# A MoE layer on one core: first rows of expert 2 moved ahead, and down products of row block pairs by seven products

## The chip, the core and the metric

One core of a Trainium2 chip. The time is the device time in microseconds of one execution. The engines named below are TensorE (PE; its weight loads are shown as PEld), VectorE (DVE), ScalarE (ACT), GpSimd (POOL) and SyncE (SP), which here only issues transfers.

## The reference

Input x is 8 sequences of 512 tokens with 256 numbers each, in f32. Two residual layers follow, and all weights are f32.

```python
# layer 1: attention, a convolution over the sequence, and attention again with the result as query
x = x + attn(layernorm(x))
# layer 2, on z = layernorm(x), returned as a whole and added to x:
h = z + attention(rmsnorm(z))          # 16 heads, rotary positions, causal
y = h + moe(rmsnorm(h))
def moe(x):                            # 8 experts, 2 per token, hidden width 704
    probs = softmax(x @ w_router)
    topw, topi = top_k(probs, 2); topw = topw / sum(topw)
    combine = sum(one_hot(topi) * topw)
    g = silu(einsum('td,xdh->txh', x, wg)); u = einsum('td,xdh->txh', x, wu)
    eo = einsum('txh,xhd->txd', g * u, wd)
    return einsum('txd,tx->td', eo, combine)
```

The change touches only the MoE. The kernel computes for each expert only the tokens that chose it.

## The kernel before

**Stages.** Up to about 865 us the kernel works through the attention layers of the eight batches. As a batch is routed, its rows are scattered by POOL (indirect DMAs, L1877) into a table `xtab` in DRAM, which has 1152 places (CAP) for each expert. Then, for each expert, rows are loaded from the table, multiplied, and added into the output by indirect DMAs from POOL (`send`, L985 to L1006). A row holds 256 numbers, its token number and its shares.

**Half experts.** An expert's rows are worked in two halves: (e, 0) has 512 rows, four row blocks of 128; (e, 1) has 608 rows, four blocks and one of 96. `places` (L2201) is the order of the halves: (0,0), then (1,0), (1,1), (2,0), (2,1) and so on to (7,1), and (0,1) last. Expert 0's first half and most of (1,0) are interleaved with the last two batches. `load_rows` (L796) is given to SP one place ahead; the rows of (1,1) can be read only when all scatters have landed. The first halves of experts 0 and 1 are read earlier, and the kernel counts with `early` and `needed` (L1134, L1858 to L1861, L1025) that enough rows of them were there; otherwise another, general path is taken at the end.

**A half.** `make(n)` transposes the rows on TensorE (L859, L866), and ScalarE brings them out of PSUM (L862, L872). `mixed_rows` adds them up in four combinations on VectorE. Then five groups k = 0..4 of 128 hidden columns, and a tail of 64. A group (L908 to L946) computes gate and up together, a 2x2 block product, by seven products instead of eight, named p1, p6, p5, p7, p1, p5, p7 in their order; each of p1, p5, p7 is read by VectorE or ScalarE between its first and its second product, which adds into the same PSUM bank. VectorE makes u, v, v and then c12, u; ScalarE makes the silu; POOL multiplies into `hT` (L943, L944). A group is cut in two by `yield`, so that other work can stand in the middle. The weights' combinations come from `mixed_weights` (eight VectorE operations per expert).

**Down products.** In the loop over n (L2246), group k of half n has in its middle `down(k)` of half n-1 (L969): one row block, six matmuls 128x256 over the hidden dimension into a PSUM bank ("bank": two of "mm", two of "av", in turn). ScalarE multiplies by the row's share (L983). The tail of half n comes after group 4. `spare` puts a few of the waiting VectorE operations after each part. POOL sends two row blocks at k = 1, one each at k = 2 and 3, and the fifth at the end. The last send of a half waits until the others have landed, and the next half's first waits for that one (`unordered`, L729).

**What sets the order.** PE, ACT, DVE and POOL run in the order in which the program lists their work (a manual schedule, L2046); SP's transfers are placed by the planner. The tiles are few: four PSUM banks "g0" to "g3" for groups and tail in turn, two buffers of p, three of u, two of v, two sets of weights (experts of even and odd number), three of rows.

Of the kernel before, what the change touches and what calls it, by code (L numbers as in the profile page):

```python
# [11 lines left out]
F32 = mybir.dt.float32  # L12
I32 = mybir.dt.int32
AF = mybir.ActivationFunctionType
ALU = mybir.AluOpType
# [679 lines left out]
def fast_path(  # L695
# [118 lines left out]
    def mixed_weights(gu, mixed):  # L814
# [13 lines left out]
            ]  # L828
        return ops

    class Half:


# [135 lines left out]
        def down(self, s):  # L969
# [12 lines left out]
            to = self.shares[s] = self.share[:m, s % 2, :]  # L982
            nc.scalar.mul(to, po, self.share_of(s)[:m])  # L983

        def send(self, n=1):  # L985

            for _ in range(n):
                s = len(self.sent)
                m = self.rows[s][1]
                self.sent.append(  # L990
                    nc.gpsimd.indirect_dma_start(  # L991
                        out=out,
                        out_offset=bass.IndirectOffsetOnAxis(
                            ap=self.rows[s][0][:m, D : D + 1].bitcast(I32), axis=0
                        ),
                        in_=self.shares[s][:m],
                        in_offset=None,
                        bounds_check=B * S - 1,
                        oob_is_err=False,
                        compute_op=ALU.add,  # L1000
                    ).ins
                )
# [40 lines left out]
    with ExitStack() as att:  # L1043
# [86 lines left out]
        for e in range(NE):  # L1130
            nc.gpsimd.memset(order[:, e : e + 1], float(NE - e))
            nc.gpsimd.memset(run[:, e : e + 1], float(e * CAP))
            nc.gpsimd.memset(limit[:, e : e + 1], float((e + 1) * CAP))
        for i, n in enumerate((FIRST, FIRST, CAP + FIRST)):  # L1134
            nc.gpsimd.memset(needed[:, i : i + 1], float(n))
        token = wp.tile([P, NT], I32, tag="token", name="token")
        nc.gpsimd.iota(token, pattern=[[P, NT]], base=0, channel_multiplier=1)
# [321 lines left out]
        class Batch:  # L1459
# [383 lines left out]
            def slots(self):  # L1843

                b = self.b
                at = small.tile(full, F32, tag="at", name="at", bufs=2)
                slot = small.tile([P, NC, 2], I32, tag="slot", name="slot", bufs=3)
                rest, red, rows = self.rest, self.red, self.rows

                ps = mm_tile()  # L1850
                n = NC * NE
                flat = self.both.rearrange("p c e -> p (c e)")
                nc.tensor.matmul(ps[:, :n], before, flat, start=True, stop=True)
                nc.tensor.matmul(ps[:, n : 2 * n], every, flat, start=True, stop=True)
                for c in range(NC):
                    nc.vector.tensor_tensor(at[:, c, :], run, ps[:, c * NE : (c + 1) * NE], ALU.add)
                    nc.vector.tensor_tensor(run, run, ps[:, n + c * NE : n + (c + 1) * NE], ALU.add)
                if b == B - 3:  # L1858
                    nc.vector.tensor_copy(early[:, 0:1], run[:, 0:1])
                if b == B - 2:  # L1860
                    nc.vector.tensor_copy(early[:, 1:3], run[:, 0:2])  # L1861

                nc.vector.tensor_tensor(rest, at, limit.unsqueeze(1).to_broadcast(full), ALU.is_ge)
                nc.vector.scalar_tensor_tensor(at, rest, float(2 * NE * CAP), at, ALU.mult, ALU.add)
                for k, pick in enumerate(self.pick):
                    nc.vector.tensor_mul(pick, pick, at)  # L1866
# [179 lines left out]
        with tc.manual_schedule(  # L2046
# [26 lines left out]
            def room(what):  # L2073
                i = next(turns_of[what])
                if what[:7] == "weights":
                    if what not in rooms:
                        first = what == "weights0"
                        gu = [
                            pool.tile([P, 2 * HID], F32, tag=tag, name="gu", bufs=1)
                            for pool, tag in (  # L2080
                                ((wp, "conv"), (wp, "wqkv_sb"))
                                if first
                                else ((big, "kT1"), (wp, "va1"))
                            )
                        ]
# [4 lines left out]
                        mixed_dn = None  # L2090
                        rooms[what] = gu, mixed, dn, mixed_dn
                    return rooms[what]
                if what == "rows":
# [19 lines left out]
                    return small.tile([P, S], F32, tag="t0", name="u", bufs=3)  # L2113
                if what == "v":
                    return wp.tile([P, S], F32, tag=("cosT", "sinT")[i % 2], name="v")
                if what == "share":
                    return big.tile([P, 2, D], F32, tag=f"cs{i % 2}", name="share")
                if what == "pgu":
# [79 lines left out]
            load_up(1, weights[1][0])  # L2198
            load_down(1, weights[1][2])
            t.rms()  # L2200
            places = [(0, 0)] + [(e, i) for e in range(1, NE) for i in range(2)] + [(0, 1)]  # L2201
            rows = {1: load_rows(room, *places[1])}
            half.tail()
            while any(due.values()):
                for where in due:
                    follow_up(where)
# [37 lines left out]
            spare(of_rows, 4)  # L2244
            halves[1].tail()
            for n in range(2, len(places) + 1):  # L2246
# [2 lines left out]
                if n + 1 < len(places):  # L2249
                    rows[n + 1] = load_rows(room, *places[n + 1])  # L2250
                if n == 2:
                    to_mix += mixed_weights(*weights[2][:2])
                if now and n > 2 and i == 0:
                    more = (e + 1) % NE
                    load_up(more, weights[more][0])
                    next_mix = mixed_weights(*weights[more][:2])
                if now and n > 2 and i == 1:
                    to_mix, next_mix = next_mix, []
                for k in range(NK - 1):
                    if now:  # L2260
                        group = now.group(k)
                        next(group)
                        spare(to_mix, 2)
                    if k == 2 and n + 1 < len(places):
                        of_rows = make(n + 1)
                    if k < len(done.rows):
                        done.down(k)
                    if k in (1, 2, 3):
                        done.send(2 if k == 1 else 1)
                    if now:  # L2270
                        next(group)
                        spare(to_mix, 1)
                    if k == 2:
                        to_mix += of_rows if n + 1 < len(places) else []
# [4 lines left out]
                if now and n > 2 and i == 0:  # L2279
# [54 lines left out]
```

## Time and profile before

| | us |
|---|---|
| median of three runs (1397.76 to 1402.78) | 1398.43 |
| the profiled execution | 1395.17 |
| its span, first to last instruction | 1393.4 |

The mean granted TensorE clock of this execution is 0.991 of full speed. The slices of the page for the other engines, 40 of 34.8 us each:

```profile
PEld 5566555666555566556565564558777878778775
DVE  5754896875896765886665865335645454544541
ACT  4677777777777776786776785323233333333331
POOL 3344334556334556333555334324444454544444
PEclk9999999999999999999999999989999999999998
```

Each digit is the busy share in tenths; PEclk is the granted clock. The MoE alone begins near slice 25. A group of instructions in the views below is given with its line, engine, operation, tiles (out<-in), shape and count. Durations of matmuls overlap[...]; the distance between starts is what one costs. A matmul in f32 has two records in the trace.

### The profile page before, as it was taken

The page shows a single profiled execution, that of the slowest core. Times are in us where ns is not written, and L with a number is a line of the kernel's source. Part 1 is how long each engine was busy: PE and PEld are TensorE (multiplying, and loading weights), DVE is VectorE, ACT ScalarE, POOL GpSimd, SP SyncE. Part 2 cuts the span into 40 slices and gives each one's busy share as a digit, 9 for nine tenths or more (in the row PEclk, how much of TensorE's full clock was granted, in tenths as well). Part 3 has the DMA queues.
Part 4 walks back from the last instruction along what each step waited for, and adds up shares of the span by engine and source line. Part 5 has one row for each costly group of instructions (what it writes and reads, how often), then busy time and mean ns, then how long its engine had stood idle before and what let it go on. Part 6 is the DMA issues. An engine that isn't in the chain of part 4 may idle for free. (4 is left out here: it accounts for less than half of the span.)

```text
span 1393.4 us, 33183 instructions
## 1 busy us (share of the span) xinstructions
PE 1338.5 (96%) x13564; PEld 908.6 (65%) x13564; DVE 856.9 (61%) x1760; ACT 789.4 (57%) x1346; POOL 628.2 (45%) x637
## 2 busy tenths in 40 slices
PE   8999999999999999999999999879999999999997
PEld 5566555666555566556565564558777878778775
DVE  5754896875896765886665865335645454544541
ACT  4677777777777776786776785323233333333331
POOL 3344334556334556333555334324444454544444
PEclk9999999999999999999999999989999999999998
DMA  5222122211001211001212023423232333333211
GB/s 143 70 83 87 67 79 82 74 40 60 17 25 55 75 43 59 13 25 39 84 50 86 13 88 93 127 53 74 57 73 55 89 85 70 73 59 79 56 17 21
DMA packets 65281, 88.50 MB, mean 64 GB/s; under 512 B 12640, under 2 KB 46624, under 8 KB 65120
## 3 DMA queue, kind: packets, MB, share of 16 engines
q1 hardware_dynamic: 51840, 68.94, 14.9%
q0 software_dynamic: 13280, 17.35, 7.4%
q8 instruction: 108, 1.77, 0.6%
q14 instruction: 53, 0.43, 0.1%
HBM read 36.35 MB, written 31.82 MB: 49 GB/s over the span
## 5 line engine op out<-in xcount | busy, mean ns | idle before, releaser
L1423 ACT ACTIVATE pr<-sc 128x1024 f32<-128x1024 f32 x432 | 418.8, 1024 | 136.9 <-PE sc L1416 131.7
L1431 POOL TENSOR_TENSOR pr<-pr,seen 128x512 f32<-128x512 f32 (+1 forms) x216 | 257.5, 1192 | 390.2 <-ACT pr L1423 380.8
L1346 PE MATMUL av<-pr,va 64*32 64x512 f32 (+7 forms) x6144 | 216.3, 407 | 0.0
L1416 PE MATMUL sc<-qT,kT 32*128 32x320 f32 (+7 forms) x2048 | 192.5, 434 | 6.4 <-ACT pr L1423 6.3
L1346 PEld LDWEIGHTS av<-pr,va 64*32 64x32 f32 x6144 | 112.1, 106 | 101.5 <-issue 78.2
L1376 DVE RECIPROCAL r<-r 128x256 f32<-128x256 f32 x96 | 167.4, 1744 | 9.8 <-DMA r<-cs 9.8
L923 PE MATMUL pgu<-xgT,gu 128*128 128x304 f32 (+1 forms) x560 | 170.7, 403 | 0.0
L1416 PEld LDWEIGHTS sc<-qT,kT 32*128 32x128 f32 x2048 | 116.2, 184 | 80.9 <-ACT pr L1423 34.5
L812 DVE TENSOR_TENSOR u<-u,pgu 128x304 f32<-128x304 f32 (+1 forms) x140 | 62.9, 449 | 167.9 <-PE pgu L923 160.7
L991 POOL DMA_INDIRECT out_dram<-share,xg x64 | 102.7, 1605 | 138.0 <-ACT share L983 129.9
L812 POOL TENSOR_TENSOR hT<-p,u 128x304 f32<-128x304 f32 (+1 forms) x70 | 80.0, 1142 | 129.7 <-DVE u L812 129.7
L923 PE MATMUL pgu<-xgT,mixed 128*128 128x304 f32 (+1 forms) x420 | 135.6, 404 | 0.4 <-DVE v L812 0.4
L923 PEld LDWEIGHTS pgu<-xgT,gu 128*128 128x128 f32 x560 | 105.6, 190 | 31.4 <-issue 3.3
L973 PE MATMUL po<-dn,hT 128*128 128x256 f32 (+1 forms) x444 | 102.1, 380 | 0.0
L973 PE MATMUL mm<-dn,hT 128*128 128x256 f32 (+1 forms) x420 | 97.0, 380 | 1.6 <-ACT xgT L862 1.6
L1416 PE MATMUL sc<-q2T,kT 32*128 32x512 f32 (+7 forms) x1024 | 93.0, 434 | 0.7 <-ACT pr L1423 0.5
L923 PEld LDWEIGHTS pgu<-xgT,mixed 128*128 128x128 f32 x420 | 78.4, 190 | 21.5 <-DVE hT L812 3.5
L973 PEld LDWEIGHTS po<-dn,hT 128*128 128x128 f32 (+1 forms) x444 | 82.0, 186 | 13.9 <-issue 0.2
L936 ACT ACTIVATE p<-pgu 128x304 f32<-128x304 f32 (+1 forms) x70 | 28.5, 407 | 108.1 <-PE pgu L923 104.0
L973 PEld LDWEIGHTS mm<-dn,hT 128*128 128x128 f32 (+1 forms) x420 | 78.3, 188 | 15.3 <-ACT xgT L862 2.9
L1877 POOL DMA_INDIRECT xtab<-rows,slot x64 | 64.9, 1014 | 35.5 <-DVE pick L1866 18.9
L1416 PEld LDWEIGHTS sc<-q2T,kT 32*128 32x128 f32 x1024 | 58.3, 184 | 32.6 <-issue 14.4
(210 smaller groups left out, 1967.7 us busy)
## 6 DMA issues: line engine op xcount, KB each, us to landing
r<-cs SPq DMA_DIRECT2D x96, 128.0 KB, 2.0
xtab<-pad SPq DMA_DIRECT2D x24, 397.5 KB, 3.5
xg<-xtab SPq DMA_DIRECT2D x16, 530.0 KB, 3.7
gu<-in_wg_dram SPq DMA_DIRECT2D x18, 352.0 KB, 4.5
cs<-cs SPq DMA_DIRECT2D x48, 128.0 KB, 1.9
gu<-in_wu_dram SPq DMA_DIRECT2D x18, 320.0 KB, 3.9
dn<-in_wd_dram SPq DMA_DIRECT2D x9, 640.0 KB, 5.1
out_dram<-x SPq DMA_DIRECT2D x8, 512.0 KB, 3.0
```

The costliest lines, as they stand in the source:

```text
L812: engine.tensor_tensor(out, a, b, op)
L923: nc.tensor.matmul(ps, lhsT, rhs, start=start, stop=True, skip_group_check=not start)
L936: nc.scalar.activation(p, p1, AF.Silu)
L973: nc.tensor.matmul(po, self.hidden(k)[:, s * P : s * P + m], self.dn[:, k, :], start=(k == 0), stop=(k == NK - 1),)
L991: nc.gpsimd.indirect_dma_start(out=out, out_offset=bass.IndirectOffsetOnAxis(ap=self.rows[s][0][:m, D : D + 1].bitcast(I32), axis=0), in_= ...
L1346: nc.tensor.matmul(av[i][g * HP : (g + 1) * HP, j * KB :], v[rows, j, ch * G + g, :], pr[rows, g, at : at + n], start=(j == 0), stop=(j == ...
L1376: nc.vector.reciprocal(r[:, half], r[:, half])
L1416: nc.tensor.matmul(sc[:, g - g0, at : at + S - j * KB], kT[r0 : r0 + HP, ch, j], qT[r0 : r0 + HP, ch, j * KB : S], start=True, stop=True,)
L1423: nc.scalar.activation(pr[:, g0 : g0 + 2], sc, AF.Exp, scale=SCALE)
L1431: nc.gpsimd.tensor_tensor(diag, diag, seen.unsqueeze(1).unsqueeze(1).to_broadcast([P, G, len(parts), KB]), ALU.mult,).ins
L1877: nc.gpsimd.indirect_dma_start(out=xtab, out_offset=bass.IndirectOffsetOnAxis(ap=slot[:, c, k : k + 1], axis=0), in_=rows[:, c, :], in_off ...
```

## The change

The order of places becomes (0,0), (1,0), (2,0), (1,1), (2,1), (3,0) and on as before. The rows of (1,0) and (2,0) are loaded together, before the last batch is routed; the counts that are asked of early rows become those of experts 0, 1 and 2. Expert 2's weights are loaded and mixed earlier, expert 1's weights are mixed one half later, and expert 3's are loaded at turn 4.

From turn 3 to turn 15 the row blocks 0 to 3 of the half before are taken in pairs. Two row blocks by the two halves of the hidden dimension (3 x 128 each) are multiplied with `wd`'s four quarters by seven products of 3 matmuls 128x128x128. Four sums of the hidden values per pair (`mixed_hidden`) and four of `wd` per expert (`mixed_down`) are made first. The pairs stand in groups 1 and 3, a fifth row block in group 4; row blocks are sent one each at k = 1 to 4. The tail moves from behind group 4 to behind group 0.

```diff
+    def mixed_down(dn, mixed):
+        t1, t2, t3, t4 = (mixed[:, n] for n in range(4))
+        b11, b12 = dn[:, :3, :P], dn[:, :3, P:]
+        b21, b22 = dn[:, 3:, :P], dn[:, 3:, P:]
+        return [
+            lambda: tt(nc.gpsimd, t1, b12, b11, ALU.subtract),
+            lambda: tt(nc.gpsimd, t2, b22, t1, ALU.subtract),
+            lambda: tt(nc.gpsimd, t3, b22, b12, ALU.subtract),
+            lambda: tt(nc.gpsimd, t4, b21, t2, ALU.subtract),
+        ]
...
+        def mixed_hidden(self, pair):
+            engine = (nc.vector, nc.gpsimd)[pair]
+            two_each = [self.room("hs") for _ in range(2)]
+            s = self.hs[pair] = [t[:, n] for t in two_each for n in range(2)]
...
+            a11, a21, a12, a22 = h1[:, :, one], h1[:, :, two], h2[:, :, one], h2[:, :, two]
+            return [
+                lambda: tt(engine, s[0], a21, a22, ALU.add),
+                lambda: tt(engine, s[1], s[0], a11, ALU.subtract),
+                lambda: tt(engine, s[2], a11, a21, ALU.subtract),
+                lambda: tt(engine, s[3], a12, s[1], ALU.subtract),
+            ]
+        def down_pair(self, pair):
...
+            p1, p6, p5, p7 = (self.room("bank")[:, :P] for _ in range(4))
...
+            def product(ps, lhsT, rhs, start=True):
+                for k in range(3):
+                    nc.tensor.matmul(ps, lhsT[:, k], rhs[:, k], start=(start and k == 0), stop=(k == 2), ...)
+            product(p1, side(h1, one), b11)
+            nc.scalar.copy(p, p1)
+            product(p6, s2, t2)
+            tt(nc.vector, u, p, p6, ALU.add)
+            product(p5, s1, t1)
+            tt(nc.vector, v, u, p5, ALU.add)
+            product(p7, s3, t3)
+            tt(nc.vector, share[:, 1, P:], v, p7, ALU.add)
+            product(p1, side(h2, one), b21, False)
+            nc.scalar.mul(share[:, 0, :P], p1, w1)
+            product(p5, s4, b22, False)
+            tt(nc.vector, share[:, 0, P:], u, p5, ALU.add)
+            nc.scalar.mul(share[:, 0, P:], share[:, 0, P:], w1)
+            product(p7, side(h2, two), t4, False)
+            tt(nc.vector, share[:, 1, :P], u, p7, ALU.add)
+            nc.scalar.mul(share[:, 1, :], share[:, 1, :], w2)
...
-        for i, n in enumerate((FIRST, FIRST, CAP + FIRST)):
+        for i, n in enumerate((FIRST, CAP + FIRST, 2 * CAP + FIRST)):
...
-                    nc.vector.tensor_copy(early[:, 1:3], run[:, 0:2])
+                    nc.vector.tensor_copy(early[:, 1:3], run[:, 1:3])
...
-            places = [(0, 0)] + [(e, i) for e in range(1, NE) for i in range(2)] + [(0, 1)]
-            rows = {1: load_rows(room, *places[1])}
+            places = [(0, 0), (1, 0), (2, 0), (1, 1), (2, 1)]
+            places += [(e, i) for e in range(3, NE) for i in range(2)] + [(0, 1)]
+            rows = {n: load_rows(room, *places[n]) for n in (1, 2)}
             half.tail()
+            load_up(2, weights[2][0])
...
-            load_up(2, weights[2][0])
             load_down(2, weights[2][2])
-            rows[2] = load_rows(room, *places[2])
-            to_mix = mixed_weights(*weights[1][:2])
+            to_mix = mixed_weights(*weights[2][:2])
             halves[1].plain_group(2)
+            spare(to_mix, 4)
+            of_rows = make(2)
             halves[1].plain_group(3)
             spare(to_mix, 4)
-            of_rows = make(2)
...
+                more = 3 if n == 4 else (e + 1) % NE
+                fresh = now and (n == 4 or n > 4 and i == 0)
+                if fresh:
                     load_up(more, weights[more][0])
                     next_mix = mixed_weights(*weights[more][:2])
...
+                pairs = now and n > 2
...
+                mix_down = {2: 2, 3: 1, 5: 3}.get(n, more if now and n > 5 and i == 1 else None)
...
                 for k in range(NK - 1):
                     if now:
                         group = now.group(k)
                         next(group)
-                        spare(to_mix, 2)
+                        spare(to_mix, 1)
                     if k == 2 and n + 1 < len(places):
                         of_rows = make(n + 1)
-                    if k < len(done.rows):
-                        done.down(k)
-                    if k in (1, 2, 3):
+                    if not pairs:
+                        if k < len(done.rows):
+                            done.down(k)
+                    elif k in (1, 3):
+                        done.down_pair(k // 2)
+                    elif k == 4 and len(done.rows) > 4:
+                        done.down(4)
+                    if not pairs and k in (1, 2, 3):
                         done.send(2 if k == 1 else 1)
                     if now:
                         next(group)
-                        spare(to_mix, 1)
...
+                        if k == 0:
+                            now.tail()
+                        if pairs and k == 0:
+                            spare(done.mixed_hidden(0), 4)
+                            spare(done.mixed_hidden(1), 4)
+                        else:
+                            spare(to_mix, 2)
+                    if pairs and k in (1, 3):
+                        done.send(1)
+                    if pairs and k in (2, 4):
+                        done.send(1)
+                    if k > 1:
+                        spare(downs, 2)
+                    to_mix += of_rows
...
                 spare(to_mix, len(to_mix))
-                if now:
-                    now.tail()
                 done.send(len(done.rows) - 4)
```

`hs` has four buffers of two sums each, `sums` two buffers of three 128x128 tiles; `mixed_dn` is one tile for each of the two weight sets.

More of the change, by code (lines that the diff above doesn't have):

```diff
@@ L983, in down @@
             nc.scalar.mul(to, po, self.share_of(s)[:m])
+        def mixed_hidden(self, pair):
+            engine = (nc.vector, nc.gpsimd)[pair]
+            two_each = [self.room("hs") for _ in range(2)]
+            s = self.hs[pair] = [t[:, n] for t in two_each for n in range(2)]
+            one = slice(2 * pair * P, (2 * pair + 1) * P)
+            two = slice((2 * pair + 1) * P, (2 * pair + 2) * P)
+            h1, h2 = self.hT[0], self.hT[1]
+            a11, a21, a12, a22 = h1[:, :, one], h1[:, :, two], h2[:, :, one], h2[:, :, two]
[5 more added lines that the diff above has]
+            ]
@@ new lines, in down_pair, with side @@
+        def down_pair(self, pair):
+            one, two = 2 * pair, 2 * pair + 1
+            h1, h2 = self.hT[0], self.hT[1]
+            def side(h, s):
+                return h[:, :, s * P : (s + 1) * P]
+            s1, s2, s3, s4 = self.hs[pair]
+            t1, t2, t3, t4 = (self.mixed_dn[:, n] for n in range(4))
+            b11, b21, b22 = self.dn[:, :3, :P], self.dn[:, 3:, :P], self.dn[:, 3:, P:]
+            p1, p6, p5, p7 = (self.room("bank")[:, :P] for _ in range(4))
+            sums = self.room("sums")
+            p, u, v = (sums[:, n, :] for n in range(3))
+            share = self.room("share")
+            w1, w2 = self.share_of(one), self.share_of(two)
+            def product(ps, lhsT, rhs, start=True):
+                for k in range(3):
+                    nc.tensor.matmul(
+                        ps,
+                        lhsT[:, k],
+                        rhs[:, k],
+                        start=(start and k == 0),
+                        stop=(k == 2),
+                        skip_group_check=not start,
+                    )
+            product(p1, side(h1, one), b11)
[14 more added lines that the diff above has]
+            nc.scalar.mul(share[:, 1, :], share[:, 1, :], w2)
+            self.shares[one], self.shares[two] = share[:, 0, :], share[:, 1, :]
@@ L2089, in room @@
                         nc.gpsimd.memset(dn[:TAIL, HT, :], 0.0)
-                        mixed_dn = None
+                        pool, tag, bufs = (wp, "va0", 1) if first else (big, "pr", 5)
+                        mixed_dn = pool.tile([P, 4, 3, P], F32, tag=tag, name="mixed_dn", bufs=bufs)
                         rooms[what] = gu, mixed, dn, mixed_dn
@@ L2115, in room @@
                     return wp.tile([P, S], F32, tag=("cosT", "sinT")[i % 2], name="v")
+                if what == "sums":
+                    return big.tile([P, 3, P], F32, tag="r", name="sums")
+                if what == "hs":
+                    return keep.tile([P, 2, 3, P], F32, tag="x", name="hs", bufs=4)
                 if what == "share":
@@ L2251, in fast_path @@
                 if n == 2:
-                    to_mix += mixed_weights(*weights[2][:2])
-                if now and n > 2 and i == 0:
-                    more = (e + 1) % NE
+                    to_mix = mixed_weights(*weights[1][:2])
+                more = 3 if n == 4 else (e + 1) % NE
+                fresh = now and (n == 4 or n > 4 and i == 0)
+                if fresh:
                     load_up(more, weights[more][0])
                     next_mix = mixed_weights(*weights[more][:2])
-                if now and n > 2 and i == 1:
+                if now and n > 4 and i == 1:
                     to_mix, next_mix = next_mix, []
+                pairs = now and n > 2
+                of_rows = []
+                mix_down = {2: 2, 3: 1, 5: 3}.get(n, more if now and n > 5 and i == 1 else None)
+                if mix_down is None:
+                    downs = []
+                else:
+                    downs = mixed_down(*weights[mix_down][2:])
                 for k in range(NK - 1):
@@ L2271, in fast_path @@
                         next(group)
-                        spare(to_mix, 1)
-                    if k == 2:
-                        to_mix += of_rows if n + 1 < len(places) else []
+                        if k == 0:
[3 more added lines that the diff above has]
+                            spare(done.mixed_hidden(1), 4)
+                        else:
+                            spare(to_mix, 2)
[6 more added lines that the diff above has]
+                    to_mix += of_rows
+                    of_rows = []
+                    if k == 1 and n == 4:
+                        to_mix, next_mix = next_mix, []
                 spare(to_mix, len(to_mix))
-                if now:
-                    now.tail()
                 done.send(len(done.rows) - 4)
-                if now and n > 2 and i == 0:
+                if fresh:
                     load_down(more, weights[more][2])
```

## The prediction

> **What bounds the kernel now.** I read the shares and slices of the page first, then the MoE stretch by stage, then TensorE in order of time, then groups by shape.
>
> ```profile
> PE 1338.5 (96%) x13564; PEld 908.6 (65%) x13564; DVE 856.9 (61%) x1760; ACT 789.4 (57%) x1346; POOL 628.2 (45%) x637
> ...
> PE   8999999999999999999999999879999999999997
> ```
>
> TensorE is the bound everywhere but in two dents, one at its end and one in slices 26 to 28. The windows (us of PE, PEld, DVE, ACT, POOL, then granted clock, DMA share, GB/s) of the second dent, and of one later half expert, show why:
>
> ```profile
> 900.90:914.00 13.10, 0.04 (x1) 0.00 (x0) 2.87 (x5) 0.00 (x0) 5.37 (x6) 0.63 0.40 110
> 914.00:917.50 3.50, 3.47 (x12) 2.63 (x13) 0.00 (x0) 1.84 (x4) 0.00 (x0) 0.50 0.39 149
> ...
> 1149.00:1180.00 31.00, 30.66 (x142) 25.33 (x141) 13.12 (x29) 10.27 (x25) 14.60 (x15) 1.00 0.34 81
> ```
>
> In a half expert TensorE has no free time and every other engine has half of it. So what TensorE saves there is won, and what makes it wait there is lost. TensorE in order of time (start, us until the last one ends, count, and the idle time before it):
>
> ```profile
> 886.74 0.39 PE L1854 MATMUL mm<-both,every 128*128 128x32 f32 x2
> 886.96 13.98 PE L897 MATMUL pgu<-xgT,gu 128*128 128x512 f32 x32
> 914.03 1.97 PE L859 MATMUL mm<-ident,xg 128*128 128x128 f32 x8 [13.09 <-DMA xg<-xtab]
> ...
> 937.45 1.04 PE L859 MATMUL mm<-ident,xg 128*128 128x128 f32 x8
> 938.32 2.75 PE L973 MATMUL po<-dn,hT 128*128 128x256 f32 x12
> 940.91 0.68 PE L923 MATMUL pgu<-xgT,mixed 128*128 128x304 f32 x2
> ```
>
> [...]A down product's row block is 12 records in 2.59 us, 0.216 each (six matmuls in f32, two records each). A 304-wide product is two in 0.51.
>
> **Part A: first rows of expert 2 before the rest of expert 1.** Before, the rows of (1,1) are loaded only when the last batch's scatters have landed: POOL issues the last at 907.9, SP issues the row load at 910.4, TensorE gets it at 914.0. It waits 13.09 us, and then runs 3.5 us at a granted clock of 0.50 and 3.5 at 0.94: 3.5 x 0.50 + 3.5 x 0.06 = 1.96 us more. The rows of (2,0) are loaded with those of (1,0) at about 869, behind scatters that are already out, so (2,0) takes the idle place; (1,1) is asked for three group turns later, near 922, and its rows land near 914 as before. What the step moves with it: six weight loads of expert 2 (SP shows them already at 870 to 873), eight mixing operations, which go to a VectorE that was busy 2.87 of those 13.1 us, and expert 3's loads, which now have one half expert (30 us) before use where others have two; six loads of some 4 us each, side by side, are covered by that; uncovered they would cost up to 8. A VectorE burst of three left-over mixing operations at the end of (2,1) may cost 1 us or so. **A gives 15.0 us.** That it only moves the wait is a rival below.
>
> **Part B, gain on TensorE.** Thirteen half experts (the turns 3 to 15) compute two pairs each by products: 7 x 3 matmuls 128 wide, 42 records, in place of 2 x 12 of 256. No row has a 128-wide f32 product with full weights. From below: the transposes at 937.45 are 128 wide, each with its own weights, 0.87/8 = 0.109 apart. From above: the 32-wide pair at 886.74, whose stream is short, so that only the weight load can pace it, is 0.11 apart. I take 0.1105: 42 x 0.1105 = 4.64 against 24 x 0.216 = 5.18. Saved 0.54 a pair, 26 pairs: **14.1 us** (12.5 to 15.6). Here a rule speaks against the change: the Trainium skill, "TensorE: Matmul & The Clock Gate", Part 3, "The mechanism", says a weight load overlaps running matmuls only where its row group differs. Load (by its "LDWEIGHTS", 128/1.2 = 107 ns) and stream would then add up to 0.216 for each 128-wide record, an estimate: 42 x 0.216 = 9.07, a loss of 3.9 a pair, 101 us in all. The transposes at 0.109, full rows, contradict it; I follow the row.
>
> **Part B, what it adds elsewhere.** Per pair: five VectorE operations on PSUM 128 wide, near 0.29 us by the slope of 421 (256) and 470 (304), and on ScalarE some 0.4 us more; both hide, each product lasting 0.66. Per half: four additions of 384 on VectorE (mixed_hidden of pair 0) and four on POOL (pair 1), and four more on POOL per expert. By shape (count, busy us, mean ns):
>
> ```profile
> L812 POOL TENSOR_TENSOR hT<-p,u 128x304 f32<-128x304 f32 x40 | 47.6, 1190 | 71.8 <-DVE u L812 71.8
> L812 DVE TENSOR_TENSOR u<-u,pgu 128x304 f32<-128x304 f32 x80 | 37.6, 470 | 82.5 <-PE pgu L923 78.5
> ...
> L812 DVE TENSOR_TENSOR xgT<-xgT 128x304 f32<-128x304 f32 x32 | 20.3, 639 | 0.3
> ...
> L812 DVE TENSOR_TENSOR mixed<-gu 128x384 f32<-128x384 f32 x16 | 9.0, 566 | 0.0
> ```
>
> VectorE needs 0.55 for 384; POOL, 0.83 for 304 undisturbed and 0.73 for 256, about 1.0. They hide as busy time. They do not hide as a queue. mixed_hidden stands on VectorE after the tail and ahead of group 1's additions and of down_pair's. The sixth product of down_pair (p5 again, with s4) adds into the bank that the pair's second addition (v) has yet to read, so TensorE waits for that whole queue, and all later products wait behind it.
>
> Worked for a 256-wide half whose POOL is on time, from TensorE's start of group 0. Group 3.02 and tail 1.72: 4.74. VectorE ends the tail's product at 6.25, then 4 x 0.55 and two dependent gaps of 0.10: 8.5. Group 1's three: 10.0. Two of the pair: 10.7. TensorE, unhindered, wants that bank at 4.74 + 2.16 + 5 x 0.66 = 10.2. Stall 0.5 to 1.0.
>
> Two things make it more. **First, the two engines' additions collide.** The same time on VectorE and POOL:
>
> ```profile
> 952.88 1.38 DVE L812 TENSOR_TENSOR xgT<-xgT 128x256 f32<-128x256 f32 x2
> ...
> 953.11 0.88 POOL L812 TENSOR_TENSOR hT<-p,u 128x304 f32<-128x304 f32 x1 [1.85 <-DVE u L812]
> 953.94 1.01 POOL L812 TENSOR_TENSOR hT<-u,v 128x304 f32<-128x304 f32 x1
> ```
>
> The first VectorE operation takes 0.42, the second 1.05: it ends 0.28 after POOL's ends. That fits the skill's "SBUF — State Buffer", "Who interferes with whom" (two SBUF inputs on VectorE against a GpSimd read: one blocks for the other's whole instruction), while operations with a PSUM input stay at 470. By the rule each of the four takes turns with a POOL one of 1.0: 4 x 1.35 instead of 2.3, 2 to 3 us a half more. By the rows a VectorE addition that meets POOL waits about half of POOL's (639 mean against 470 alone; 890 in the bad ones). I take half.
>
> **Second, POOL is late in five halves.** After a half with five row blocks POOL sends row blocks 4 and 5 back to back, and the last send waits until the others have landed:
>
> ```profile
> 1370.84 1.46 POOL L991 DMA_INDIRECT out_dram<-share,rest  x1
> 1374.62 1.58 POOL L991 DMA_INDIRECT out_dram<-share,xg  x1 [2.32 <-issue]
> ```
>
> 3.8 us from one issue to the next. So POOL: hT of group 4 until 2.4, send 4 until 4.1, send 5 from 6.4 to 7.9, hT of group 0 until 8.8. In a 304-wide half the tail's second part needs the p buffer that this reads (two buffers), so VectorE ends the tail at 9.9 instead of 6.9, p7 of group 1 starts at 10.0 instead of 7.2, and with mixed_hidden behind it the pair's bank comes free at 15.2 (no collision) or 18.1 (full turns) against 11.5: 3.7 or 6.6 us.
>
> Stalls without and with full turns: turns 6, 8, 10, 12, 14: 5 x 3.7 or 6.6; turns 7, 9, 11, 13: 4 x 1.0 or 3.2; turns 4 and 15: 2 x 1.4 or 4.2; turn 5: 2.5; turn 3: 0.7 or 3.3. Sum 28 or 60. I take the middle, 44. If POOL or VectorE had room that I don't see, this term falls, below neither zero.
>
> **Sum.** -15.0 - 14.1 + 44 = +15 us. The profiled execution took 1395.17 (span 1393.4): 1410. The median of the three runs is 3.3 above it: **1414**. The ends of the stalls give -1 and +31: 1397 and 1429. 0.5% (7 us) is about what a measurement can tell from no change.
>
> **Rivals.**
> 1. *VectorE keeps up*: the mixing fits in the idle half of both engines (13.1 and 14.6 busy of 31 us), stalls come to 14 instead of 44. For it: the busy shares, and that the tail was put ahead as cover. Against: the queue order above. -29 + 14 = -15: **1383**. With no stall at all, 1369.
> 2. *Full turns*: the collision is as the rule says: **1429**.
> 3. *A only moves the wait*: rows of (2,0) land late or expert 3's weights do, and 15 us stay: 1429. For it: SP has both row loads in one queue. Against: that queue is empty between 874 and 885. (If the new counts failed, the general path would run and take far longer; batch 7 of 8 should have given each expert some 896 rows of 512 asked.)
> 4. *Weight loads add up*: 1500, against the 0.109 of the transposes.
>
> **Chances.** Forecast 0.30, rival 2 0.17, rival 3 0.05, rival 4 0.02: slower 0.54 (own range 1406 to 1432). Rival 1: faster 0.36. The end without collision, where all cancels (1397): within 0.5%, 0.10. The range runs from rival 1 with a little more, 1377, to 1434.
>
> **What would show it.** A: no gap over 1 us on TensorE between 887 and 960, clock 1.00 there. B: 42 records of a pair in 4.6 us plus waits; waits of TensorE on VectorE at the first pair's sixth product in each half, longest in the 304-wide halves after five row blocks; mixed_hidden on VectorE near 0.9 mean, not 0.55. If the hs additions show 0.55 and the half takes 30 us or less, rival 1 is right. If 128-wide records stand 0.2 apart, rival 4.

## The result and the profile after

| | us |
|---|---|
| before, median (1397.76 to 1402.78) | 1399.17 |
| after, median (1470.33 to 1474.17) | 1473.75 |
| ratio after / before, 95% interval | 1.0514 [1.0481, 1.0547] |
| profiled execution of after; its span | 1470.33; 1468.6 |

The kernel became 5.1% slower. The forecast was 1414 (1377 to 1434): slower was right, the size was not. The page of after, rows of shares and slices:

```profile
PE 1360.9 (93%) x14032; PEld 923.0 (63%) x14032; DVE 990.8 (67%) x1942; ACT 802.8 (55%) x1398; POOL 729.7 (50%) x725
...
PE   8999999999999999999999989978989888888886
```

A slice is 36.7 us here. The old dent's time, 887 to 922, lies in slices 25 and 26, and both are at 9; from slice 27 on, where the pairs begin, most are at 8 or 7 instead of 9. No engine is full; TensorE has become one that waits. In order of time (start, us until the last one ends, count, idle before), TensorE at the old dent, and then in turn 10:

```profile
891.60 0.39 PE L1929 MATMUL mm<-both,every 128*128 128x32 f32 x2
891.82 10.55 PE L909 MATMUL pgu<-xgT,gu 128*128 128x512 f32 x24
902.20 1.04 PE L871 MATMUL mm<-ident,xg 128*128 128x128 f32 x8
903.08 7.03 PE L909 MATMUL pgu<-xgT,gu 128*128 128x512 f32 x16
909.95 1.88 PE L967 MATMUL pgu<-xgT,gu 128*128 128x512 f32 x4
911.66 0.59 PE L935 MATMUL pgu<-xgT,gu 128*128 128x256 f32 x2
...
1217.10 0.68 PE L935 MATMUL pgu<-xgT,gu 128*128 128x304 f32 x2
1220.38 0.78 PE L935 MATMUL pgu<-xgT,mixed 128*128 128x304 f32 x2 [2.60 <-DVE hT L812]
1221.00 0.92 PE L935 MATMUL pgu<-xgT,gu 128*128 128x304 f32 x2
1221.71 1.49 PE L1033 MATMUL mm<-dn,hT 128*128 128x128 f32 x6
```

Turn n of the loop computes half n in the order of places, so turn 2 is (2,0) here and (1,1) before. From the last batch's `every` to the first group of turn 2 it is 911.66 - 891.60 = 20.1 us, with no wait in between, against 922.29 - 886.74 = 35.6 before: part A took 15.5. The loss is in the loop from there to the end: 471.1 us before, 556.9 after.

I sorted these times by the distance between the starts of neighbouring matmuls: the usual distance of its shape is work; what is above it counts as clock where the granted clock is half, and else as a stall. So the split between clock and stalls is a reading of the trace, good to a microsecond or so.

| us | before | after |
|---|---|---|
| work | 450.2 | 438.0 |
| half clock | 0 | 14.2 |
| stalls | 10.9 | 92.4 |
| of them: ahead of group 1's fourth product (p7), turns 6, 8, 10, 12, 14 | 0 | 17.6 |
| of them: products of a half's first pair | 0 | 25.5 |
| of them: all others | 10.9 | 49.3 |

The expectations below count the wait ahead of p7 as group 1's third product. The last 2.7 us of the difference stand behind the last matmul; what caused them was not looked for. The other 4.8 us to the span's 75.2 come before the change's place: 1.5 in attention, 3.3 at 853 to 866, where the clock fell to 0.75 behind the same wait of 3 us as before. The traces of all later versions have half clock at this place as well; that the profiled execution of before has none there is luck.

What the other engines did there, POOL and VectorE in order of time, turn 10 (the sends of the fourth and fifth row blocks, then products of group 0, then sums for the second pair; beside it the tail's second part and the sums for the first pair):

```profile
1212.93 1.58 POOL L1066 DMA_INDIRECT out_dram<-share,xg  x1 [0.15 <-issue]
1217.06 1.45 POOL L1066 DMA_INDIRECT out_dram<-share,rest  x1 [2.55 <-DMA out_dram<-share,xg]
1218.01 1.36 POOL L812 TENSOR_TENSOR hT<-p,u 128x304 f32<-128x304 f32 x1
1218.79 1.35 POOL L812 TENSOR_TENSOR hT<-u,v 128x304 f32<-128x304 f32 x1
1219.58 1.51 POOL L812 TENSOR_TENSOR hs<-hT 128x384 f32<-128x384 f32 x1
...
1215.70 0.47 DVE L812 TENSOR_TENSOR hT<-p,pgu 64x304 f32<-64x304 f32 x1 [0.90 <-ACT p L975]
1219.85 0.47 DVE L812 TENSOR_TENSOR hT<-p,pgu 64x304 f32<-64x304 f32 x1 [3.67 <-ACT p L975]
1220.36 1.16 DVE L812 TENSOR_TENSOR hs<-hT 128x384 f32<-128x384 f32 x1
1221.55 1.23 DVE L812 TENSOR_TENSOR hs<-hs,hT 128x384 f32<-128x384 f32 x1
1222.71 1.35 DVE L812 TENSOR_TENSOR hs<-hT 128x384 f32<-128x384 f32 x1
```

This is the chain that the prediction wrote out: two sends, late hT, a p buffer that comes free only then, the tail 4.15 us apart in its two parts, and hs at 1.2 to 1.35 us each. And at the end of the same turn stands one that it lacked:

```profile
1247.07 1.57 POOL L1066 DMA_INDIRECT out_dram<-share,xg  x1 [0.16 <-issue]
1248.10 1.57 POOL L812 TENSOR_TENSOR mixed_dn<-dn 128x384 f32<-128x384 f32 x1
1249.07 1.54 POOL L812 TENSOR_TENSOR mixed_dn<-dn,mixed_dn 128x384 f32<-128x384 f32 x1
...
1247.66 3.24 DVE L812 TENSOR_TENSOR xgT<-xgT 128x256 f32<-128x256 f32 x1
1250.83 1.03 DVE L812 TENSOR_TENSOR u<-u,pgu 128x304 f32<-128x304 f32 x2
```

An addition that takes 0.42 elsewhere takes 3.24: it starts as POOL sends, and ends 0.3 after the second of two sums of `wd`, which stood behind the send and waited for nothing. The additions of the groups stand behind it; turn 11 begins with 2.06 us of waiting. The largest single waits outside the two named kinds are in turn 4, at group 0 and at its end:

```profile
987.24 1.38 PE L935 MATMUL pgu<-xgT,mixed 128*128 128x304 f32 x2 [4.02 <-DVE v L812]
1024.98 0.19 PE L1113 MATMUL mm<-good,all_one 128*1 128x2 f32 x2 [3.64 <-DVE all_one L1112]
```

By the distances between starts they are 4.19 and 3.80 us, against 0.53 and 1.43 before. Ahead of the first, VectorE makes the check of the sums' range, 18 small operations from 981.8 to 986.2; ahead of the second, what is left of the mixing of rows, four operations in 2.68 us.

### The profile page after: what moved, and what is told of

The parts are those of the page before. It is cut to its first block, busy times and chain, and to the rows that moved or that the text cites. A ratio compares the mean times of both kernels' runs of the same rounds, so it can differ in the third digit from the quotient of the medians.

```text
span 1468.6 us, 34584 instructions
## 1 busy us (share of the span) xinstructions
PE 1360.9 (93%) x14032; PEld 923.0 (63%) x14032; DVE 990.8 (67%) x1942; ACT 802.8 (55%) x1398; POOL 729.7 (50%) x725
## 5 line engine op out<-in xcount | busy, mean ns | idle before, releaser
L1421 PE MATMUL av<-pr,va 64*32 64x448 f32 (+7 forms) x6144 | 219.4, 407 | 0.0
L935 PE MATMUL pgu<-xgT,gu 128*128 128x304 f32 (+1 forms) x560 | 176.8, 414 | 12.1 <-DVE u L812 12.1
L935 PE MATMUL pgu<-xgT,mixed 128*128 128x304 f32 (+1 forms) x420 | 142.2, 421 | 25.4 <-DVE hT L812 16.8
L812 POOL TENSOR_TENSOR hT<-p,u 128x304 f32<-128x304 f32 (+1 forms) x70 | 64.2, 916 | 183.0 <-DVE u L812 182.9
L935 PEld LDWEIGHTS pgu<-xgT,gu 128*128 128x128 f32 x560 | 105.8, 193 | 49.7 <-DVE u L812 15.7
L935 PEld LDWEIGHTS pgu<-xgT,mixed 128*128 128x128 f32 x420 | 75.0, 193 | 53.2 <-DVE hT L812 22.8
L1491 PEld LDWEIGHTS sc<-q2T,kT 32*128 32x128 f32 x1024 | 58.3, 184 | 32.6 <-issue 14.2
L812 POOL TENSOR_TENSOR hT<-u,v 128x304 f32<-128x304 f32 (+1 forms) x70 | 67.3, 962 | 0.0
L1331 PE MATMUL mm<-xT,wqkv_sb 128*128 128x512 f32 x128 | 62.5, 615 | 3.9 <-DMA wqkv_sb<-in_wqkvT_dram 2.7
L1717 DVE TENSOR_TENSOR t<-t,mm 128x256 f32<-128x256 f32 x32 | 12.0, 417 | 76.7 <-ACT t L1712 76.7
L812 DVE TENSOR_TENSOR hT<-p,pgu 64x304 f32<-64x304 f32 (+2 forms) x34 | 20.0, 588 | 64.6 <-ACT p L975 44.0
```

What stands on the lines that cost most here:

```text
L812: engine.tensor_tensor(out, a, b, op)
L935: nc.tensor.matmul(ps, lhsT, rhs, start=start, stop=True, skip_group_check=not start)
L1331: nc.tensor.matmul(ps, w[:, d, n0 : n0 + P], srcT[:, d, :S], start=(d == 0), stop=(d == DC - 1),)
L1421: nc.tensor.matmul(av[i][g * HP : (g + 1) * HP, j * KB :], v[rows, j, ch * G + g, :], pr[rows, g, at : at + n], start=(j == 0), stop=(j == ...
L1491: nc.tensor.matmul(sc[:, g - g0, at : at + S - j * KB], kT[r0 : r0 + HP, ch, j], qT[r0 : r0 + HP, ch, j * KB : S], start=True, stop=True,)
L1717: nc.vector.tensor_tensor(t[:, i], m1, ps[:, 1], op)
```

## The experiments

All runs are compared with runs of the kernel before on the same chip (medians 1400.9 to 1402.4). "Against after" is the difference of the ratios times 1399. What was expected of each, theory and rivals, stands ahead of its result.

### Each part alone

The order of places, rows, weights and counts, with the rest as before:

```diff
-                pairs = now and n > 2
+                pairs = False
...
-                        if k == 0:
-                            now.tail()
...
+                if now:
+                    now.tail()
                 done.send(len(done.rows) - 4)
```

> The order of places, rows, weights and counts as in the changed kernel; down products by row block, tail and spare operations as before. Theory 1 (the two parts are independent, and part A took the 15.5 us that the trace of after shows between the last batch and the first group of (2,0)): 1384 us, no stall of TensorE over 1 us between the last batch and turn 3. Theory 2 (the earlier rows and the later loads of expert 3 cost something further on, which the pairs' stalls cover up in after): 1390 or more, with the loss in turns 4 to 6.

Measured: 1385.77, ratio 0.9888 [0.9871, 0.9904], 15.7 us faster than before; the clock was full from turn 2 to 15, and the waits 11.9 us in all against 10.9 before. Theory 1. The other half, pairs on the places of before (`mixed_down` for expert 1 in turn 2, for 2 in turn 3, then one half expert after another):

> The pairs, their sums and the tail behind group 0 on the places of before; nothing of the reorder. Theory 1 (independent parts; everything that was lost, was lost by the pairs): 1474 + 15 = 1489 us, the idle 13 us after the last batch back in their place. Theory 2 (a good part of the loss is the reorder's, or the clock's after another start): 1465 or less.

Measured: 1483.4, ratio 1.0585 [1.0568, 1.0603]. 1.0585 - 0.0112 = 1.0473 is what independent parts would give for both, and both gave 1.0514: they add up to within 0.4%, which is about what the intervals of the three ratios leave open. The loss is the pairs'.

### The sums of wd

```diff
-                mix_down = {2: 2, 3: 1, 5: 3}.get(n, more if now and n > 5 and i == 1 else None)
+                mix_down = {2: 2, 3: 1}.get(n)
```

> As after, but POOL makes the four sums of wd for experts 2 and 1 only; the later experts take the sums that stand there, so this leaves out computation. Theory 1 (VectorE's additions without a PSUM input are held while one of POOL's sums of wd runs or is queued behind a send; what they hold up is the next groups' additions): the VectorE additions of rows and weights at k = 2 to 4 go back from 2.3 and 3.3 us to below 1.1, TensorE's waits of 2.0 us at the start of turns 7, 9, 11, 13 and 15 shrink to 0.5, those of 0.6 at groups 3 and 4 of the even turns and the 3.2 of turn 15 go, in all some 17 us and a little clock: 1452 us. Theory 2 (POOL has half its time free, its sums hide; the waits come from the pairs themselves): 1468 or more.

Measured: 1455.62, ratio 1.0373 [1.0346, 1.0399]: 20 us against after, 7 of them in turn 15. The sums of turns 2 and 3 are still made. By shape (count, busy us, mean ns), turns 4 to 15, of after and then of this run:

```profile
L812 DVE TENSOR_TENSOR xgT<-xgT 128x256 f32<-128x256 f32 x20 | 22.6, 1140 | 0.2
...
L812 DVE TENSOR_TENSOR mixed<-gu,mixed 128x256 f32<-128x256 f32 x6 | 11.9, 1986 | 0.0
```

```profile
L812 DVE TENSOR_TENSOR xgT<-xgT 128x256 f32<-128x256 f32 x20 | 11.4, 579 | 0.2
...
L812 DVE TENSOR_TENSOR mixed<-gu,mixed 128x256 f32<-128x256 f32 x6 | 2.5, 419 | 0.0
```

Nothing of VectorE's work was changed; 1986 ns became 419. Theory 1. Of the waits of 2.05 at the start of turns 7, 9, 11 and 13 nothing is left there, but a wait of some 1.3 came up at group 1 of these turns, where one of VectorE's hs now takes up to 2.84 us beside POOL. The 0.56 at group 4 of the even turns stayed, against theory 1: these are not POOL's doing.

The same four sums made by VectorE at the same places:

```diff
-            lambda: tt(nc.gpsimd, t1, b12, b11, ALU.subtract),
+            lambda: tt(nc.vector, t1, b12, b11, ALU.subtract),
```

> As after, but VectorE makes the four sums of wd at the same places in the program. Theory 1 (what costs is that VectorE's additions take turns with POOL's sums, also with those queued behind a send): most of what leaving them out gave comes back although VectorE has 2.3 us an expert more: 1457 us, VectorE's additions at k = 2 to 4 below 1.1 us each. Theory 2 (what costs is the work at this place in whatever queue): the additions queued ahead of the groups' own hold them up as before, 1467 or more.

Measured: 1467.96, ratio 1.0488 [1.0468, 1.0507]: 4 us against after, less than the two intervals can tell from nothing; that is theory 2's time. Its VectorE in order of time at the end of turn 10:

```profile
1244.91 1.39 DVE L812 TENSOR_TENSOR xgT<-xgT 128x256 f32<-128x256 f32 x2
1246.22 1.18 DVE L812 TENSOR_TENSOR mixed_dn<-dn 128x384 f32<-128x384 f32 x1
1247.32 0.55 DVE L812 TENSOR_TENSOR mixed_dn<-dn,mixed_dn 128x384 f32<-128x384 f32 x1
1247.78 0.46 DVE L812 TENSOR_TENSOR u<-p,pgu 128x304 f32<-128x304 f32 x1
```

The 3.24 is gone, as theory 1 says (xgT 128x256 is back at 578 ns), but four operations in a row before a group's first addition hold it up as well: TensorE waits 2.13 us at group 4 in turns 6, 8, 10 and 12. The collision makes the operations long; the place makes it a stall. Both have to go.

### The sums of hidden values

Left out:

```diff
-                lambda: tt(engine, s[0], a21, a22, ALU.add),
...
+            self.hs[pair] = [a22, a21, a11, a12]
+            return []
```

> As after, but the four sums of hidden values of each pair are left out: the products take blocks of the hidden values as they are, so this leaves out computation. Theory 1 (the waits at the first pair's products are those for these sums, slowed by turns of VectorE and POOL, and for what is queued behind them): of some 2 to 3 us in each of 13 half experts, below 0.7 stays: 25 us less, 1447. TensorE's waits of 2.8 to 4.5 us at group 1's third product in turns 6, 8, 10, 12 and 14 stay, since the tail's p buffer sets these. Theory 2 (the waits belong to the pair's own chain of banks: copy, addition, addition, and the product that comes back to the bank): 1465 or more.

Measured: 1447.43, ratio 1.0317 [1.0299, 1.0334]: 28 us. All waits at the first pair were gone; the pair's own chain of banks costs nothing there, theory 2 is out. The five waits at group 1 stayed, 2.7 to 4.6 us. And with the sums in, but the second pair's one group later:

```diff
                             spare(done.mixed_hidden(0), 4)
-                            spare(done.mixed_hidden(1), 4)
...
+                        if pairs and k == 1:
+                            spare(done.mixed_hidden(1), 4)
```

> As after, but POOL makes the second pair's four sums one group later, behind group 1, so that VectorE's four for the first pair do not meet them. Theory 1 (full turns: each of VectorE's sums waits for one of POOL's): VectorE's hs go from 1.3 to 0.6 or 0.7 us each, the waits at the first pair from 2 to 3 us to below 1.2: 1455 us. Theory 2 (POOL's products of group 0 and its sends slow VectorE's sums just as much): hs stay above 1.1 us, 1467 or more.

Measured: 1452.78, ratio 1.0370 [1.0352, 1.0389]: 20 us. By shape, VectorE's and POOL's sums in after, then here:

```profile
L812 POOL TENSOR_TENSOR hs<-hT 128x384 f32<-128x384 f32 x24 | 32.0, 1332 | 0.0
...
L812 DVE TENSOR_TENSOR hs<-hT 128x384 f32<-128x384 f32 x24 | 28.7, 1196 | 0.4
```

```profile
L812 POOL TENSOR_TENSOR hs<-hT 128x384 f32<-128x384 f32 x24 | 24.0, 1001 | 0.0
...
L812 DVE TENSOR_TENSOR hs<-hT 128x384 f32<-128x384 f32 x24 | 13.3, 555 | 0.4
```

VectorE's became as short as its additions of this size are alone, and POOL's shorter too. The waits at the first pair went to 0.36 at most, from 25.5 to about 1 us in all: almost all that was lost there was the meeting of the two engines and not the work. The whole gain is less, since waits at the second pair, where POOL's sums now stand, grew from 7 to 14 us: 1.2 in turns 6, 8, 10 and 12, and 6.9 in turn 15.

### The tail and the sends

The tail behind group 4 again:

> As after, but the tail stands behind group 4 again, as before the change. Theory 1 (group 1 waits in turns 6, 8, 10, 12 and 14 because the tail behind group 0 needs a p buffer that POOL, late from two sends, still reads): the five waits of 2.8 to 4.5 us at group 1's third product go, 17 us, and some 5 us of clock; the sums of the first pair lose the 1.7 us of cover that the tail gave, and the waits at the first pair grow by 0.5 to 1 us a half: 1460 us. Theory 2 (the tail as cover is worth its whole length): first pair's waits grow by 1.7 us in each of 13 half experts, which takes back all: 1472 or more. Theory 3 (the first pair's waits are from the tail's delay itself): they shrink too, 1445.

Measured: 1433.92, ratio 1.0237 [1.0205, 1.0269]: 39 us, beyond all three, nearest to theory 3. The five waits went, as theory 1 says. But the waits at the first pair did not grow for lack of cover: they shrank from 25.5 to 18.6 us. VectorE, without the tail before it, begins its sums at once and makes one or two of them undisturbed (0.55) before POOL begins with its own; in turn 9 these start at 1162.0 on VectorE and at 1164.1 on POOL. In after the tail delays VectorE until both run side by side. With both engines' sums at this place the tail was no cover; it lined them up. That is not so where POOL's sums stand later: with the tail left ahead (the run before) VectorE's took 0.555 and the first pairs waited about 1 us in all, and with the tail behind group 4 as well (the three moves together, below) VectorE's met POOL's products of group 0, took 0.55 to 1.18 us in turn 10, and the first pairs waited 5.5. With the tail left where the change put it, and the fifth send in the next half:

```diff
+                        if k == 0 and late is not None:
+                            late.send(len(late.rows) - 4)
...
-                done.send(len(done.rows) - 4)
+                if pairs and n + 1 < len(places):
+                    late = done
```

> As after, but the fifth row block is sent in the next half expert, on POOL behind the sums at k = 0, so that POOL does not stand between two sends while group 0's products wait. Theory 1 (POOL's lateness after the fourth and fifth send holds the p buffer): the five waits of 2.8 to 4.5 us at group 1's third product shrink below 0.5, and the half clocks after them go: 17 us and some 5 of clock less, 1448 us. Theory 2 (the two p buffers are too few for a tail behind group 0 whatever POOL does): 1467 or more.

Measured: 1454.42, ratio 1.0379 [1.0356, 1.0402]: 19 us, and no wait left ahead of group 1's p7 above 0.3: theory 1 by the mechanism. By the size it fell 6 us short of its 1448; the waits at the first pair grew by some 4 us.

### Together

> As after, with the tail behind group 4 again, the second pair's sums one group later, and the fifth row block sent in the next half. Theory 1 (three stalls with causes of their own, their gains add up less what two of them share): of the tail's 37 us, some 15 more by the later sums and little more by the later send, which mends what the tail's move has mended already: 1415 us; VectorE's hs below 0.65 us each, the waits at the first pair below 0.5. Theory 2 (the gains overlap fully: whichever is taken first wins the queue its time back): 1430 or more.

Measured: 1420.36, ratio 1.0154 [1.0133, 1.0176]: 50 us, where the three single gains come to 78. That is nearer to theory 1 than to theory 2, with an overlap of 28. VectorE's hs did not come below 0.65 as expected: 0.84 and, where they read hs first, 1.03 on the mean. What was left: 0.6 to 1.3 us at pairs and around groups 4 and 0, 3.1 and 2.8 in turn 4, and 6.9 in turn 15, where POOL makes the sums of the tile of odd experts once more, for nobody, when the second pair is about to read it. The later sums and the later send with the tail left ahead were not tried together. So:

```diff
-                mix_down = {2: 2, 3: 1, 5: 3}.get(n, more if now and n > 5 and i == 1 else None)
+                mix_down = {2: 2, 3: 1}.get(n, e if now and n > 4 and i == 0 else None)
...
+                        if k > 0:
+                            spare(one_each, 2 if k == 1 else 1)
```

> As the three moves together, and the sums of wd on VectorE, one or two in a place, in first halves of an expert where it has no weights to mix (turn 2 stays on POOL), none in turn 15; weights and rows are mixed two and one in a place as before the change. Theory 1 (what is left are waits of 0.5 to 1 us behind the mixing at k = 3 and 4 and at the next group 0, and the 3 to 7 us of turn 15): 20 us less than the three moves alone, 1395 us. Theory 2 (pairs that cost no wait anywhere): TensorE's saving of 12.5 us shows against the reorder alone, 1375. Theory 3 (VectorE is too full for it; sums in any place hold up a group): 1410 or more.

Measured: 1405.75, ratio 1.0048 [1.0026, 1.0069]: 15 us less than the three moves, between theories 1 and 3. TensorE waited 1.2 us at nearly every first pair and 0.3 to 1.1 at the second; one or two mixing operations stood just before each. Without these:

```diff
+                        some = one_each or to_mix
+                        if not pairs:
+                            spare(some, 2 if k else 1)
+                        elif k in (0, 2, 4):
+                            spare(some, 0 if k == 0 and one_each else 2 if k else 1)
...
-                if n == 3:
+                    if n == 2 and k == 0:
                         good = sums_in_range()
```

> As the run before (sums of wd spread on VectorE), but no mixing operation stands on VectorE in the places just ahead of a pair (first half of groups 1 and 3), and the check of the sums' range moves from turn 3 to turn 2, which has no pairs. Theory 1 (the 1.2 us at every first pair and 0.3 to 1.1 at every second are the one or two mixing operations that stand before the pair's own additions in VectorE's queue): 16 and 8 us go, and some 3 of turn 4: 1380 us, below the reorder alone (0.9888 of before). Theory 2 (the operations only move, and the groups that they now stand before wait instead): 1400 or more.

Measured: 1391.83, ratio 0.9937 [0.9914, 0.9960]: 15.5 us less again, faster than before, but 7 behind the reorder alone, and between the two theories. The waits at the first pair went, as theory 1 says, and so did the one at turn 4's group 0, with the check moved; small ones came up in the groups instead, as theory 2 says (0.2 and 0.4 at group 3). Its loop has 25.6 us of stalls and 1.6 of clock against 11.9 and 0, some 15 more, to pay for 12.5 of work. What is left is below 0.7 us a place but for 1.2 in turn 2 and 2.8 at the end of turn 4, where the reorder alone has 2.5. The best of all versions is the order of places without pairs, 1385.77.

## Why the prediction missed

**Part A: right.** 15.0 forecast, 15.5 in the trace, 15.7 alone. The rows of (2,0) were there, the loads of expert 3 came in time, rival 3 is out.

**Part B on TensorE: right.** 128-wide records stand 0.112 apart (0.1105 taken), as 1186.94 - 1186.27 = 0.67 for six in turn 9:

```profile
1186.27 0.83 PE L1033 MATMUL po<-mixed_dn,hs 128*128 128x128 f32 x6
1186.94 0.83 PE L1033 MATMUL mm<-mixed_dn,hs 128*128 128x128 f32 x6
1189.22 0.91 PE L1033 MATMUL po<-dn,hT 128*128 128x128 f32 x6 [1.45 <-ACT sums L1043]
```

42 x 0.112 = 4.70 a pair, a saving of 0.48, 12.5 us instead of 14.1. The Trainium skill, "TensorE: Matmul & The Clock Gate", Part 3, "The mechanism", lets a weight load overlap running matmuls only where its row group differs, from which the prediction estimated 0.216; for these full-row f32 products the trace contradicts that, and rival 4 is out.

**Stalls that were named: right by sum, wrong in the choice behind it.** 44 were forecast for group 1 and the first pairs; 17.6 + 25.5 = 43.1 came. But the prediction wrote "By the rows a VectorE addition that meets POOL waits about half of POOL's", and "I take half". The four sums for the first pair took 1196 to 1235 ns each against 555 alone: nearer to the 1.35 us that the working had for full turns than to the 0.96 of half turns. This agrees with the Trainium skill, "SBUF — State Buffer", "Who interferes with whom": a VectorE instruction with two SBUF inputs contends with a GpSimd one that reads SBUF, and the lock is exclusive. The half was a mean over single additions, of which 18 of 32 had met nobody (0.47 us); most of the others waited 0.42. Four in a row beside four of POOL's waited 0.64 to 0.68 each. With full turns the working had 6.6 us for each of turns 6, 8, 10, 12 and 14, where waits and half clock together came to 6.1 to 7.7, and 3.2 for turns 7, 9, 11 and 13, where 2.3 to 3.2 came. That the sum of stalls still fits 44 instead of 60 is luck: the clock took its share of the waiting, and turns 4 and 15 had 2.8 instead of 8.4. The place was one product off as well. The prediction had TensorE wait for VectorE at the pair's sixth product; some 14 of the 25.5 us were at the fifth, as at 1189.22 above. It waits for ScalarE's copy of p1, which stands behind group 1's silu, which waited for VectorE:

```profile
1188.53 0.38 ACT L948 ACTIVATE p<-pgu 128x256 f32<-128x256 f32 x1 [5.50 <-DVE u L812]
1188.82 0.26 ACT L1043 COPY sums<-po 128x128 f32<-128x128 f32 x1
```

The cause is the one that was named, VectorE's queue behind mixed_hidden; the way by which it reached TensorE was mostly another.

**The step that failed** is "They hide as busy time", for the four sums of `wd`, and with it the list of stalls, which looked at k = 0 and 1 alone. These sums were named as an addition to POOL and then never put into a queue. At k = 2 to 4 they meet VectorE's mixing of rows and weights. Without those from turn 5 on the time falls by 20 us, which contains the 3.2 of the needless ones in turn 15. Mixing operations one and two in a place instead of two and one were not weighed either (0.56 at group 4 in even turns, which was gone in the run that has two and one again; that run changed other places too). For left-over mixing at the end of (2,1), which is turn 4, the prediction gave 1 us or so: with the reorder alone the wait there grew by 1.1, with the pairs by 2.4. And at turn 4's group 0, behind the check, which the prediction did not weigh, it grew by 3.7. All stalls that its sum did not have come to 49.3 - 10.9 = 38.4 us.

**A term was absent: the clock.** 14.2 us. The prediction counted 1.96 us of half clock for the wait that it removed, and none for those that it added. In turn 10 (us, busy us of PE, PEld, DVE, ACT, POOL; granted clock, DMA share, GB/s) after the wait of 2.6:

```profile
1217.00:1220.40 3.40, 0.80 (x5) 0.25 (x3) 0.52 (x2) 0.83 (x2) 3.34 (x4) 1.00 0.65 186
1220.40:1223.90 3.50, 3.50 (x15) 3.13 (x16) 3.46 (x3) 0.00 (x0) 3.42 (x4) 0.63 0.14 34
1223.90:1227.40 3.50, 2.85 (x21) 2.65 (x20) 3.26 (x7) 0.58 (x2) 1.01 (x1) 0.88 0.00 0
```

**The tail as cover was wrong in sign, as the change has it.** The working let the tail give VectorE 1.72 us of TensorE's time. Moved back, the first pairs wait 7 us less and not more, and 39 us are won in all, with the 17.6 at group 1, which the prediction did put down to the tail's p buffer.

In all, in the profiled execution: -15.5 (A) - 12.2 (work) + 43.1 (named stalls) + 38.4 (others) + 14.2 (clock) + 2.7 (end) + 4.8 (before the change) = 75.5, against 75.2 measured. The forecast had the first three. Two of its sums are off without bearing on this: its terms give 1413 and not 1414, and rival 4's 1500 leaves out A's gain and the stalls, with which it is 1528.

## What to carry to other kernels

List every operation that a change adds, and put each one into its engine's queue at its place, with what stands there at that moment on the other engine; a small one in the wrong place cost as much here as the whole reorder gained. VectorE and POOL additions with both inputs in SBUF held each other up here (1.20 us instead of 0.555 on VectorE, 1.33 instead of 1.00 on POOL): sum them up as one queue, and don't give both engines such work at once. Before adding work to the engines that stand beside a bound one, compare the gain (0.96 us of 31.5 here) with one stall; where a single wait of 1 us eats it, the margin is too small.

## What was not expected of the hardware

- A POOL addition seems to take its turn before it runs: VectorE's addition was held at 2.3 and 3.24 us through a send that stood ahead of two of POOL's. Taking these sums away cured it there. With the tail back, a sum of VectorE's for the first pair was held for 3.83 us in the same way, through a send and the two hT and one hs behind it. Where POOL's next instruction had still to wait for VectorE, as hT behind a send in the kernel before, VectorE's additions beside a send took their 0.42 to 0.47. The queued instruction was not tried apart from the send.
- In the loop of after, half clock came in windows of 3.4 or 6.8 us behind waits of TensorE of 2 us and more, but not behind each: turn 11 lost 1.5 us behind a wait of 2.06, turns 7, 9 and 13 nothing behind 2.05. The reorder alone, with no wait above 2.51 in the loop, lost nothing there. It is not in proportion: without the sums of hidden values the stalls fell from 92.4 to 65.7 us, and the clock's share rose from 14.2 to 21.0. That the waits cause it is argued from the order of events; no run held the two apart.
